# Layer 3's second product by Strassen's seven products, with the first product of the next group issued ahead of the last one of this group

## The chip, the cores and the metric

The kernel runs on one core of one Trainium2 chip. The metric is device time in microseconds (us), the median of several executions. The profiled execution of the kernel before has a span of 2726.4 us at a mean granted TensorE clock of 0.980.

Engines in the profile: PE is TensorE's matmuls, PEld its weight loads, DVE is VectorE, ACT is ScalarE, POOL is GpSimd, SP is SyncE; a "q" behind the name is that engine's instruction queue. L734 is line 734 of the kernel of that run.

## The reference

Four graph layers, each `x + layer(relu(layernorm(x)))`, on 128 graphs of 128 nodes and 256 features, in float32. Only the end of the fourth layer ("layer 3") changes:

```python
h = jax.nn.relu(_batchnorm(x @ W1.T + b1, g1, be1))   # x: 16384 rows; h: 16384 x 512
out = h @ W2.T + b2                                   # the "second product": 512 -> 256
out = _batchnorm(out, g2, be2)                        # statistics over all rows
```

Both batch normalizations need statistics over all rows, so the layer has three phases. The first product, which is merged into the main phase, writes its result `z` to HBM. The second product reads it back in 32 groups of 512 rows. The last phase (the "tail" below) normalizes, transposes, adds x and stores.

## The kernel before

The second product works on features by rows: a group `z` is 128 partitions x 4 feature blocks x 512 rows (1 MB). ScalarE applies the normalization and ReLU in place, TensorE does 2 x 4 matmuls of 512 columns, VectorE adds the bias and takes the statistics.

```python
EARLY = 6
x3p = pool("x3p", bufs=EARLY)              # x tiles for the tail, loaded ahead
zin = pool("zin", bufs=3)                  # three groups of z in SBUF
for n, g in enumerate(ORDER):
    z = ZT[g]
    for j in range(FC):                    # FC = 4
        nc.scalar.activation(z[j], z[j], AF.Relu, bias=sh1[:, j:j+1], scale=sc1[:, j:j+1])
    for i in range(DC):                    # DC = 2
        po = bank([P, T], f"po_{g}_{i}")   # T = 512 rows
        for j in range(FC):
            nc.tensor.matmul(po, bw2T[:, j, i*P:(i+1)*P], z[j], start=(j == 0), stop=(j == FC-1))
        nc.vector.tensor_scalar(O[g][:, i, :], po, b2_c[:, i:i+1], None, ALU.add)
        nc.vector.bn_stats(stats2[:, i, g, :], O[g][:, i, :])
    if n + 1 + AT_ONCE < NG: load_z(n + 1 + AT_ONCE)     # AT_ONCE = 3
    ...                                    # and sometimes one early x3 load
```

(Pool and slice notation shortened.) The weights `W2.T` are transposed in the preparation, parked in HBM as `BW2T`, and read back when the product starts.

## Time and profile before

| | before |
|---|---|
| time, median of 4 | 2728.28 us (2726.66 to 2731.1); 2727.35 of 3 when the prediction was made |
| first `h` of the kernel (end of the preparation) | 29.81 us |
| start of the second product on TensorE | 2424.80 us |
| second product, first to last matmul ("the block") | 221.95 us, 6.87 us a group |
| tail, from the block's end to the end | 79.65 us |

The last four rows cut the span into a start, a block and a tail, whose lengths add up to the span. The lines behind the table are in the prediction.

### The profile page before, as it was taken

Reading aid. Unit: us, or ns where it says so; the run is one execution under the profiler, and the core shown is the slowest. Engines: PE = TensorE matmul, PEld = TensorE weight load, DVE = VectorE, ACT = ScalarE, POOL = GpSimd, SP = SyncE. Lnnn points to the kernel's source line nnn. Section 1 sums busy time; section 2 is a strip of 40 time slices with the busy share of each in tenths; the row PEclk is TensorE's granted clock in tenths of the full one; section 3 lists DMA queues with packets and bytes.
Section 4 is the critical chain, followed back from the end, with each engine's and each line's share of the span. In section 5 each row is a group of like instructions: output and inputs, shape, how many; then the busy total and the mean of one; then the engine's idle time right before and its main releaser. Section 6 shows DMA issues by size and latency. Waiting matters only on the chain.

```text
span 2726.4 us, 38769 instructions
## 1 busy us (share of the span) xinstructions
PE 2611.4 (96%) x14703; PEld 2201.7 (81%) x14703; DVE 1806.0 (66%) x4528; ACT 1194.1 (44%) x2307; POOL 465.5 (17%) x484
## 2 busy tenths in 40 slices
PE   4899999999999999999999999999999999979994
PEld 2788888888888888888888888888888888954443
DVE  6666776676677766666777667677766665544445
ACT  2444444444444444444444444444444443334445
POOL 4111111111111111111111111111111111110001
PEclk6899999999999999999999999999999999989997
DMA  3000000000000000000000000000000000034449
GB/s 134 1 25 23 32 32 32 32 24 32 24 32 32 32 32 32 32 29 19 32 32 32 32 24 32 24 32 32 32 32 32 32 24 11 37 147 154 154 169 363
DMA packets 61756, 142.14 MB, mean 52 GB/s; under 512 B 4594, under 2 KB 39940, under 8 KB 57604
## 3 DMA queue, kind: packets, MB, share of 16 engines
q1 hardware_dynamic: 50224, 103.36, 10.7%
q0 software_dynamic: 9216, 33.56, 3.1%
q10 hardware_dynamic: 2132, 2.76, 0.3%
q8 instruction: 116, 1.90, 0.3%
q14 instruction: 68, 0.56, 0.1%
HBM read 73.08 MB, written 66.58 MB: 51 GB/s over the span
## 4 chain that ended last, share of the span: by engine, by line
PE 70%; DVE 20%; ACT 4%; POOL 3%; DMA 2%; issue 2%; ACTq 0%; DVEq 0%; POOLq 0%; SPq 0%
PE p_x L338 10%; PE po L714 8%; PE p_x L321 6%; PE p_z L338 4%; PE p_z L321 4%; PE pu_x L321 4%; PE pz_x L338 4%; DVE st L258 3%; DVE uT L280 3%; POOL rs L145 3%; PE pm L277 2%; PE p_y L338 2%; PE pg L277 2%; ACT h L267 2%; PE p_y L321 2%; PE ps L466 2%
## 5 line engine op out<-in xcount | busy, mean ns | idle before, releaser
L267 ACT ACTIVATE h<-x,sh,rs 128x256 f32<-128x256 f32 x512 | 265.9, 590 | 232.3 <-DVE sh L264 220.3
L145 POOL TENSOR_TENSOR rs<-rs,nhalf 128x4 f32<-128x4 f32 x128 | 135.1, 1056 | 1039.7 <-DVE rs L143 1039.7
L353 ACT COPY p_t<-p_x 128x512 f32<-128x512 f32 (+1 forms) x192 | 97.6, 508 | 343.1 <-PE p_x L338 340.9
L338 PE MATMUL p_x<-uT,w 128*128 128x256 f32 x1024 | 242.3, 379 | 0.0
L553 ACT ACTIVATE h2T<-h2T 128x512 f32<-128x512 f32 x192 | 119.9, 625 | 226.9 <-DVE h2T L552 226.9
L390 DVE SCALAR_TENSOR_TENSOR gs<-h,gw 128x256 f32<-128x256 f32 x384 | 203.8, 531 | 18.8 <-ACT h L267 6.8
L714 PE MATMUL po<-zi,bw2T 128*128 128x512 f32 x496 | 213.0, 592 | 0.0
L338 PEld LDWEIGHTS p_x<-uT,w 128*128 128x128 f32 x1024 | 189.7, 190 | 23.1
L258 DVE BATCH_NORM_STATS2 st<-x 128x6 f32<-128x256 f32 x512 | 191.0, 414 | 4.4 <-DMA x<-in_x_dram 2.2
L714 PEld LDWEIGHTS po<-zi,bw2T 128*128 128x128 f32 x496 | 94.2, 190 | 118.6 <-issue 108.1
L604 DVE TENSOR_TENSOR zo<-pz_z,pz_t 128x512 f32<-128x512 f32 x32 | 22.1, 691 | 185.6 <-PE pz_z L338 185.6
L707 ACT ACTIVATE zi<-zi,sh_bn,sc_bn 128x512 f32<-128x512 f32 x124 | 90.5, 802 | 116.7 <-DMA zi<-z 116.7
L718 DVE TENSOR_SCALAR o<-po,vecs 128x512 f32<-128x512 f32 x64 | 48.0, 750 | 128.7 <-PE po L714 128.7
L277 PEld LDWEIGHTS pmu<-a2T,u 128*128 128x128 f32 x1024 | 119.8, 192 | 15.0 <-PE pr L579 7.4
L338 PE MATMUL p_x<-uT,w_s 128*128 128x256 f32 x512 | 124.3, 385 | 6.1 <-DVE h2T L552 6.1
L321 PEld LDWEIGHTS p_x<-w,h2T 128*128 128x128 f32 x1024 | 124.3, 192 | 3.3
L338 PE MATMUL p_x<-us,w_s 128*128 128x256 f32 x512 | 126.0, 379 | 0.0
L321 PE MATMUL p_x<-w,h2T 128*128 128x128 f32 x1024 | 124.6, 275 | 0.0
L338 PE MATMUL p_y<-uT,w 128*128 128x256 f32 x512 | 121.1, 379 | 0.0
L338 PE MATMUL p_z<-us,w 128*128 128x256 f32 x512 | 121.0, 379 | 0.0
L338 PE MATMUL p_z<-us,w_s 128*128 128x256 f32 x512 | 121.0, 379 | 0.0
L277 PE MATMUL pmu<-a2T,u 128*128 128x128 f32 x1024 | 119.9, 275 | 0.0
(250 smaller groups left out, 5871.3 us busy)
## 6 DMA issues: line engine op xcount, KB each, us to landing
z<-zo SPq DMA_DIRECT2D x62, 512.0 KB, 2.6
zi<-z SPq DMA_DIRECT2D x31, 1024.0 KB, 4.8
x<-in_x_dram SPq DMA_DIRECT2D x32, 512.0 KB, 3.9
x<-x POOLq DMA_DIRECT2D x32, 512.0 KB, 3.0
x3i<-x POOLq DMA_DIRECT2D x32, 512.0 KB, 6.8
out_dram<-x3i SPq DMA_DIRECT2D x64, 256.0 KB, 6.6
w<-in_L_gnn_W_dram SPq DMA_DIRECT2D x1, 2048.0 KB, 11.1
bw<-in_L_gnn_W_dram ACTq DMA_DIRECT2D x2, 512.0 KB
```

The lines of the kernel that those rows point to most:

```text
L145: nc.gpsimd.tensor_tensor(dst, src, nhalf[:, : dst.shape[1]], ALU.pow)
L258: nc.vector.bn_stats(st[:, b, :], xt[:, b, :])
L267: nc.scalar.activation(h[:, b, :], xt[:, b, :], AF.Relu, bias=sh[:, b : b + 1], scale=rs[:, b : b + 1])
L277: nc.tensor.matmul(pm[:, b, :], src[:, b, c * P : (c + 1) * P], aT, start=True, stop=True)
L280: nc.vector.tensor_copy(dst[:, c, :], pm.rearrange("p b n -> p (b n)"))
L321: nc.tensor.matmul(pb[:, rr, :], a_r[r][:, c, rr * P : (rr + 1) * P], b_r[r][:, c, :wide], start=(first and rr == 0 and c == 0), stop=(c = ...
L338: nc.tensor.matmul(pb[:, jj, :], b_r[r][:, c, at : at + P], a_r[r][:, c, :], start=(first and jj == 0 and c == 0), stop=(c == nk - 1), ski ...
L353: nc.scalar.copy(t, pb)
L390: nc.vector.scalar_tensor_tensor(gs, h[:, b, :], 1.0, gw[:, i, :], ALU.mult, ALU.mult, accum_out=gl[:, b, i : i + 1],)
L553: nc.scalar.activation(dst, dst, AF.Relu)
L707: nc.scalar.activation(z[j], z[j], AF.Relu, bias=sh1[:, j : j + 1], scale=sc1[:, j : j + 1],)
L714: nc.tensor.matmul(po, bw2T[:, j, i * P : (i + 1) * P], z[j], start=(j == 0), stop=(j == FC - 1),)
```

## The change

Strassen's scheme in Winograd's form: A (the activations of one group) and B (the weights) are cut into 2 x 2 blocks, and seven products of half-sized blocks replace eight. Block sums of the weights are made once in the preparation (three extra blocks, `BW2S`, parked next to `BW2T`); block sums of the activations are made per group: S1 and S2 and the update of A12 on VectorE, the new A21 on GpSimd. The output needs sums of products too: four products are copied from PSUM by ScalarE, three added by VectorE. Of the four copies one is final and three are kept for a later sum: t1 behind product 0, t5 behind product 4, t2 behind product 5. The bias moves into the last normalization.

```diff
+    def second(g):
+        ...                                  # a11, a21, a12, a22: blocks of z; s1, s2: ex
+        a_r = a11, a12, a12, a22, s1, s2, a21
+        for j in range(FC):
+            nc.scalar.activation(z, z, AF.Relu, bias=..., scale=...)
+            yield
+        nc.vector.tensor_tensor(s1, a21, a22, ALU.add)
+        nc.gpsimd.tensor_tensor(a21, a11, a21, ALU.subtract)
+        nc.vector.tensor_tensor(s2, s1, a11, ALU.subtract)
+        yield
+        def product(r, pb, first):
+            for c in range(FC // 2):
+                nc.tensor.matmul(pb, BW2R[r][:, c, :], a_r[r][:, c, :], ...)
+            if r == 1:
+                nc.vector.tensor_tensor(a12, a12, s2, ALU.subtract)
+        ...                                  # put(): output copy or sum, statistics
+        yield from seven(product, put, [P, T // 2], f"po_{g}", zw)
     for n, g in enumerate(ORDER):
-        (ReLUs, 8 matmuls, bias, statistics: see above)
+        then = second(ORDER[n + 1]) if n + 1 < NG else iter(())
+        for _ in range(PREPARE):             # PREPARE = FC + 1
+            next(now)                        # a product of this group
+            next(then, None)                 # a ReLU, then the sums, of the next
+        next(then, None)                     # the next group's FIRST product
+        for _ in now: pass                   # this group's LAST product
+        now = then
```
```diff
-        nc.scalar.dma_start(BW2T, bw2t)
+        bw2s = prep.tile([P, 3, FC // 2, D // 2], FP, name="bw2s")
+        seven_of(bw2t, "bw2t", bw2s)         # four differences on GpSimd
+        nc.sync.dma_start(BW2T, bw2t)
+        nc.sync.dma_start(BW2S, bw2s)
...
-    EARLY = 6        (and 9 late x3 tiles)
+    EARLY, LATE = 4, 11
+    zw = pool("zw", bufs=2)                  # s1, s2 and the kept copies
```

`seven` runs the products in the order 0, 1, 4, 5, 2, 6, 3. Three PSUM banks serve them: x (0, then 5, 6 and 3 added on), y (1), z (4, then 2 added on). Product 2 reads the updated A12. And product 3 adds onto the bank that the output sum behind product 6 still reads; that is why the next group's product 0 is put between 6 and 3.

More of the change, by code (lines that the diff above doesn't have):

```diff
@@ L145, in inv_sqrt, with quarters, set_of, seven_of @@
         nc.gpsimd.tensor_tensor(dst, src, nhalf[:, : dst.shape[1]], ALU.pow)
+    def quarters(a):
+        k, t = a.shape[1] // 2, a.shape[2] // 2
+        return a[:, :k, :t], a[:, k:, :t], a[:, :k, t:], a[:, k:, t:]
+    def set_of(b, extra):
+        b11, b21, b12, b22 = quarters(b)
+        return b11, b21, b22, extra[:, 2], extra[:, 0], extra[:, 1], b12
+    def seven_of(b, name, extra=None):
+        b11, b21, b12, b22 = quarters(b)
+        if extra is None:
+            extra = weights.tile([P, 3, b.shape[1] // 2, b.shape[2] // 2], FP, name=f"{name}_s")
+        operands = set_of(b, extra)
+        t4n, t1, t2 = operands[3:6]
+        nc.gpsimd.tensor_tensor(t1, b12, b11, ALU.subtract)
+        nc.gpsimd.tensor_tensor(t2, b22, t1, ALU.subtract)
+        nc.gpsimd.tensor_tensor(t4n, b21, t2, ALU.subtract)
+        nc.gpsimd.tensor_tensor(b12, b22, b12, ALU.subtract)
+        return operands
     BW2T = scratch.tile([P, FC, D], FP, name="BW2T")
+    BW2S = scratch.tile([P, 3, FC // 2, D // 2], FP, name="BW2S")
     with tc.tile_pool(name="prep", bufs=1) as prep:
@@ L280, in mixed @@
             nc.vector.tensor_copy(dst[:, c, :], pm.rearrange("p b n -> p (b n)"))
-    def quarters(a):
-        k, t = a.shape[1] // 2, a.shape[2] // 2
-        return a[:, :k, :t], a[:, k:, :t], a[:, :k, t:], a[:, k:, t:]
-    def seven_of(b, name):
-        b11, b21, b12, b22 = quarters(b)
-        extra = weights.tile([P, 3, b.shape[1] // 2, b.shape[2] // 2], FP, name=f"{name}_s")
-        t1, t2, t4n = (extra[:, i] for i in range(3))
-        nc.gpsimd.tensor_tensor(t1, b12, b11, ALU.subtract)
-        nc.gpsimd.tensor_tensor(t2, b22, t1, ALU.subtract)
-        nc.gpsimd.tensor_tensor(t4n, b21, t2, ALU.subtract)
-        nc.gpsimd.tensor_tensor(b12, b22, b12, ALU.subtract)
-        return b11, b21, b22, t4n, t1, t2, b12
     def sums(engine, a, extra, s3=None):
@@ L344, in columns_by_half, with seven @@
         return product
-    def seven(product, put, shape, name):
+    def seven(product, put, shape, name, pool=None):
         def kept(pb, i):
-            t = w.tile(shape, FP, tag="kept", name=f"{name}_t{i}", bufs=6)
+            t = (pool or w).tile(shape, FP, tag="kept", name=f"{name}_t{i}", bufs=6)
             nc.scalar.copy(t, pb)
@@ L679 @@
     O = [keep.tile([P, DC, T], FP, name=f"o_{g}") for g in range(NG)]
-    EARLY = 6
+    EARLY, LATE = 4, 11
     x3p = ctx.enter_context(tc.tile_pool(name="x3p", bufs=EARLY, reuse_waits="tile"))
@@ L684 @@
     )
+    zw = zs.enter_context(tc.tile_pool(name="zw", bufs=2, side="right", reuse_waits="tile"))
     bw2T = keep.tile([P, FC, D], FP, name="bw2T")
     nc.scalar.dma_start(bw2T, BW2T)
+    bw2s = keep.tile([P, 3, FC // 2, D // 2], FP, name="bw2s_late")
+    nc.scalar.dma_start(bw2s, BW2S)
+    BW2R = set_of(bw2T, bw2s)
     ORDER = [LAST, *range(LAST)]
@@ L693, in load_z @@
         nc.sync.dma_start(z, Z[ORDER[n]])
-        ZT[ORDER[n]] = [z[:, j, :] for j in range(FC)]
+        ZT[ORDER[n]] = [z[:, :FC // 2, :], z[:, FC // 2 :, :]]
     def load_x3(g, pool, tag):
@@ L698, in load_x3, with put @@
         nc.gpsimd.dma_start(R[g], X3[g])
+    def second(g):
+        zl, zr = ZT[g]
+        ex = zw.tile([P, 2, FC // 2, T // 2], FP, tag="zs", name=f"zs_{g}")
+        a11, a21, a12, a22 = (z[:, :, i * T // 2 : (i + 1) * T // 2] for z in (zl, zr) for i in range(2))
+        s1, s2 = ex[:, 0], ex[:, 1]
+        a_r = a11, a12, a12, a22, s1, s2, a21
+        for j in range(FC):
+            z = ZT[g][j // 2][:, j % 2, :]
+            nc.scalar.activation(
+                z, z, AF.Relu, bias=sh1[:, j : j + 1], scale=sc1[:, j : j + 1],
+            )
+            yield
[5 more added lines that the diff above has]
+            for c in range(FC // 2):
+                nc.tensor.matmul(
+                    pb, BW2R[r][:, c, :], a_r[r][:, c, :],
+                    start=(first and c == 0), stop=(c == FC // 2 - 1), skip_group_check=True,
+                )
+            if r == 1:
+                nc.vector.tensor_tensor(a12, a12, s2, ALU.subtract)
+        done = []
+        def put(ij, pb, other):
+            i, j = ij
+            dst = O[g][:, j, i * T // 2 : (i + 1) * T // 2]
+            if other is None:
+                nc.scalar.copy(dst, pb)
+            else:
+                nc.vector.tensor_tensor(dst, pb, other, ALU.add)
+            done.append(j)
+            if done.count(j) == 2:
+                nc.vector.bn_stats(stats2[:, j, g, :], O[g][:, j, :])
+        yield from seven(product, put, [P, T // 2], f"po_{g}", zw)
     for n in range(1, 1 + AT_ONCE):
@@ L702 @@
     sc1, sh1 = bn_affine(stats1, FC, g1_c, be1_c, "bn1", b1_c)
-    ZT[LAST] = [z[:, jj, :] for z in ZT[LAST] for jj in range(2)]
+    PREPARE = FC + 1
+    now = second(LAST)
+    for _ in range(PREPARE + 1):
+        next(now)
     for n, g in enumerate(ORDER):
-        z = ZT[g]
-        for j in range(FC):
-            nc.scalar.activation(
-                z[j], z[j], AF.Relu,
-                bias=sh1[:, j : j + 1], scale=sc1[:, j : j + 1],
-            )
-        for i in range(DC):
-            po = bank([P, T], f"po_{g}_{i}")
-            for j in range(FC):
-                nc.tensor.matmul(
-                    po, bw2T[:, j, i * P : (i + 1) * P], z[j],
-                    start=(j == 0), stop=(j == FC - 1),
-                )
-            nc.vector.tensor_scalar(O[g][:, i, :], po, b2_c[:, i : i + 1], None, ALU.add)
-            nc.vector.bn_stats(stats2[:, i, g, :], O[g][:, i, :])
+        then = second(ORDER[n + 1]) if n + 1 < NG else iter(())
+        for _ in range(PREPARE):
+            next(now)
+            next(then, None)
+        next(then, None)
+        for _ in now:
+            pass
+        now = then
         if n + 1 + AT_ONCE < NG:
@@ L724 @@
     zs.close()
-    late = ctx.enter_context(tc.tile_pool(name="late", bufs=9, reuse_waits="tile"))
+    late = ctx.enter_context(tc.tile_pool(name="late", bufs=LATE, reuse_waits="tile"))
     def load_later(g):
-        load_x3(g, *((late, "x3l") if EARLY <= g < EARLY + 9 or g % 5 > 1 else (x3p, "x3")))
-    for g in range(EARLY, EARLY + 9):
+        load_x3(g, *((x3p, "x3") if g % (EARLY + LATE) < EARLY else (late, "x3l")))
+    for g in range(EARLY, EARLY + LATE):
         load_later(g)
-    sc2, sh2 = bn_affine(stats2, DC, g2_c, be2_c, "bn2")
+    sc2, sh2 = bn_affine(stats2, DC, g2_c, be2_c, "bn2", b2_c)
     for g in range(NG):
@@ L753 @@
             nc.sync.dma_start(out[at : at + 2].rearrange("b n d -> n b d"), x3[:, half, :])
-        if g + EARLY + 9 < NG:
-            load_later(g + EARLY + 9)
+        if g + EARLY + LATE < NG:
+            load_later(g + EARLY + LATE)
 _INS = [
```

## The prediction

> **What bounds the kernel now.** I read the page first (busy shares, the 40 slices, the chain of work that ended last), then the chain in order of time, the busy time of each engine by stretches, the groups of the lines concerned, and last the timeline of the three joints that the change touches: the preparation, the start of the second product, its end.
>
> From the page:
>
> ```profile
> PE 2611.4 (96%) x14703; PEld 2201.7 (81%) x14703; DVE 1806.0 (66%) x4528; ACT 1194.1 (44%) x2307; POOL 465.5 (17%) x484
> ...
> DMA  3000000000000000000000000000000000034449
> ```
>
> TensorE has work nearly everywhere, but the DMA row shows another regime in the last slices. The end of the chain in order of time separates the stages:
>
> ```profile
> 2416.91 1.80 DVE mv_bn L659 x2
> 2419.85 1.81 DVE mv_bn L659 x2
> 2424.80 221.95 PE po L714 x512
> 2650.93 15.69 ACT o L738 x23
> 2673.03 3.92 DMA x3i<-x
> ```
>
> So layer 3's second product is one unbroken TensorE block of 221.95 us, 8% of the span; behind it comes a tail of 76 us that ends in transfers. Everything ahead of 2416 us is the same code before and after, apart from the preparation. Busy time by stretches (columns PE, PEld, DVE, ACT, POOL, granted clock, DMA share, GB/s), one stretch inside the product and three of the tail:
>
> ```profile
> 2500.00:2550.00 50.00, 50.00 (x117) 22.04 (x116) 20.84 (x29) 21.76 (x30) 0.00 (x0) 1.00 0.41 147
> ...
> 2647.00:2654.00 7.00, 2.19 (x9) 1.74 (x10) 3.45 (x8) 3.07 (x5) 2.80 (x5) 0.76 0.78 270
> 2654.00:2664.00 10.00, 9.10 (x61) 7.94 (x60) 9.29 (x16) 10.00 (x15) 1.10 (x2) 0.83 0.90 297
> ...
> 2694.00:2704.00 10.00, 6.75 (x54) 6.19 (x52) 7.29 (x13) 2.19 (x4) 2.12 (x4) 0.95 1.06 404
> ```
>
> In the product TensorE is 100% busy at full clock, DVE and ACT 42 to 44%, POOL 0, DMA 41%: only TensorE binds. In the tail DMA binds: some 390 to 400 GB/s once saturated, but only 270 and 297 in its first 17 us. The groups of the product's line give the cost of one instruction:
>
> ```profile
> L714 PEld LDWEIGHTS po<-zi,bw2T x496: 190/190/190, 2433.3 to 2645.7; 128*128 128x128 f32 x166
> L714 PE MATMUL po<-zi,bw2T x496: 592/592/593, 2433.7 to 2646.1; 128*128 128x512 f32 x166
> ```
>
> (2646.1 - 2433.7)/495 = 0.429 us from one matmul to the next. A matmul of the code is two TensorE instructions (16 a group, 8 in the code), so a group takes 16 x 0.429 = 6.87 us.
>
> **What the Trainium skill says.** (1) "TensorE: Matmul & The Clock Gate", section "Back-to-back issue gap": the isolated warm gap grows with the moving columns, N/2.4 + 2.5 ns, 216 ns at 512. This trace has 429 ns at 512 columns of f32, twice that, so I take the proportionality and not the figure: eight 256-column f32 matmuls at 2227.91 us take 1.89 us, the last 0.379, hence (1.89 - 0.379)/7 = 0.216. Half the columns cost half. (2) The same page, "What's actually happening": after idle time the clock is halved for some 3.4 us. The trace agrees: after the 8 us gap ahead of the product the first weight loads are 0.86 us apart for 4.2 us. This loss stays. (3) "SBUF — State Buffer", "Who interferes with whom": a DVE instruction with two SBUF inputs and a GpSimd instruction that reads SBUF exclude each other, the later one waits. The trace agrees; beside POOL's sums at 2225.61 us the gate product takes 0.83 us in place of 0.42:
>
> ```profile
> 2225.45 0.41 DVE L390 SCALAR_TENSOR_TENSOR gs<-h,gw 128x256 f32<-128x256 f32 x1
> 2225.61 0.84 POOL L304 TENSOR_TENSOR gs<-gT 128x256 f32<-128x256 f32 x1 [5.61 <-DVE gT L280]
> ...
> 2226.77 0.82 DVE L390 SCALAR_TENSOR_TENSOR gs<-h,gw 128x256 f32<-128x256 f32 x1
> ```
>
> (4) "DMA: Bandwidth & Descriptors", "Where 436 GB/s comes from", puts HBM to SBUF at about 358 GB/s a core; the tail measures up to 404, so I use about 390.
>
> **The change part by part.**
>
> *TensorE, removed.* A group's 16 instructions of 512 columns become 7 products x 2 chunks x 2 passes = 28 of 256 columns: 28 x 0.2155 = 6.03 us against 6.87. If nothing else binds: 0.83 x 32 = 26.7 us. The weight load (0.190) still hides under the 0.216, as in the main phase.
>
> *ACT, added.* Four ReLUs (a run of four takes 2.92 us, 0.71 apart) plus four PSUM copies of 128x256 (0.35 each): about 4.2 us a group of 6.03.
>
> *DVE, replaced.* Gone: two bias additions of 0.75. New: three 128x512 sums (starts 0.60 apart) and three 128x256 sums from PSUM (0.42, or 0.35 apart); the two statistics (0.69) stay. About 4.1 us a group. No total binds; the order within a group does.
>
> *POOL, added.* One 128x512 difference a group, 1.27 us by its group in the main phase (L307).
>
> *The order.* Let product 6 of the last group end at 0; slots are 0.86 us: 0' to 0.86, 3 to 1.72, 1' to 2.58, 4' to 3.45, 5' to 4.31, 2' to 5.17, 6' to 6.03. On DVE: last output sum 0.09 to 0.50, statistics to about 1.1, s1' to 1.73 (in time for 4', which starts at 2.4), s2' to 2.33 (in time for 5'). POOL's difference needs s1' done, finds DVE in s2' (two SBUF inputs), and runs about 2.33 to 3.6. The update of a12', again two SBUF inputs, wants to start at 2.7 to 3.0 and is locked out until 3.6; it ends at 4.3. Product 2' should start near 4.15; it starts near 4.45. The loop from one product 6 to the next is then 4.45 + 0.17 (pipeline) + 2 x 0.86 = 6.35, not 6.03. The ACT order just passes: the copy t2' ends near 4.87, product 6' needs it near 4.9. I take **6.3 us a group**: (6.87 - 6.30) x 32 = **18.1 us saved**.
>
> *Transfers of z.* A buffer is now free when product 3 of its group ends, and its successor is read 6.03 + 0.4 = 6.4 us later. Before, the end of the group at about 2626.08 led to the ReLU at 2631.07: 5.0 us. There is slack of 1.4 us, so no charge.
>
> *Preparation.* The first h waits for a store of the preparation:
>
> ```profile
> 22.82 2.35 POOL L292 TENSOR_TENSOR w_s<-w 128x1024 f32<-128x1024 f32 x1
> ...
> 24.30 0.37 ACTq L237 DMA_DIRECT2D BW2T<-bw2t  x1
> ...
> 29.81 2.08 ACT L267 ACTIVATE h<-x,sh,rs 128x256 f32<-128x256 f32 x4 [12.04 <-DMA BW2T<-bw2t]
> ```
>
> Now four POOL sums of 128x256 (0.72 each here) go ahead of that store. POOL is busy until 25.17, so the trigger moves from 24.3 to about 25.2 + 2.9 = 28.1. The 5.4 us of landing before were queueing (DMA share 1.1 until 28 us, then 0.09); now two stores, 896 KB, go into an empty queue: 2 us of start and 0.9 MB at 370 GB/s, so about 32.4. The first h is 2.6 us later. TensorE binds from 60 us on, so this passes through: **+2.6 us**.
>
> *Joint at the end of the product.* The last product 3 has nothing between it and product 6: it waits for the sum that reads its bank, about 0.75. A copy of 0.37 takes the place of the 0.75 addition, -0.4; the bias in the last normalization adds two small DVE steps, 0.3. **+0.65 us**. At the start I charge nothing: in the half-clock stretch ACT keeps ahead.
>
> *Tail.* x3 loads before: 7 by 2426 us, 2 at 2633.5, 2 at 2640.4, 4 at 2647.3. After, the early pool has four buffers, not six, and by the sizes in the code the eleven late ones lie nearly all where z and its sums lie: about 1 goes 8 us ahead of the product's end, 2 go 2.6 us ahead, 8 at its end. That leaves some 4.75 loads, 2.5 MB, more for the tail. Unused bandwidth at the tail's start was (390 - 270) x 7 + (390 - 297) x 10 = 1.77 MB, which the eight waiting loads can fill. Net 0.7 MB or 1.9 us, and I allow 1 us for imperfect filling: **+3 us**.
>
> Sum: -18.1 + 2.6 + 0.65 + 3 = -11.9 us; 2727.35 - 11.9 = **2715.5 us**.
>
> **Rivals.** (a) *TensorE stays the only bound*: period 6.05, 26.2 us saved, and the rest as above: 2707. For it: the main phase runs such sevens with PE 99% busy. Against: there POOL and other streams have slack; here one stream is left. (b) *The DVE and POOL chain binds harder*: if POOL wins the lock first, s2' ends near 3.8, after product 5' wants it (3.28), and the wait repeats in every group: period 6.5 or more, 11.8 us saved or less: 2722. (c) *The gain is given back at the joints*: store, late x3 loads and tail at their worst, 5 + 6 us with 1.6 between: 2722 at period 6.3, near the time before if (b) holds too. (d) *Z transfers no longer land in time*, ACT stalls in order and the copies behind it: 0.5 us a group would cost 16 us. The 1.4 us of slack speaks against it.
>
> **Range and chances.** (a) with mild joints gives about 2705, (b) with bad joints 2724: that is the range. 2% is 54.5 us; even with all else free the gain is 26.7 us, and a loss of 54.5 would need a period above 8.2 us, more than any engine's total. So within 2% is nearly sure.
>
> **What would show it.** Right: the product's block near 202 us for 221.95, 896 matmuls about 0.216 apart with a pause of about 0.3 us a group ahead of product 2, waiting for a12 (DVE, then POOL); the first h near 32.4 us; x3 loads bunched at the product's end, DMA share 1 from there; the tail about 82 us against 79. Wrong: pauses ahead of product 5 or 6, ReLUs that wait for z, a block near 194 or above 210 us, an h that starts near 30, or a main phase of another length.

## The result and the profile after

The changed kernel takes **2716.15 us** (median of 4, 2715.21 to 2718.01) against 2728.28 us (median of 4). The ratio is 0.9955, 95% interval 0.9938 to 0.9973, well inside 2%.

The cut into stages, with the prediction's terms beside it:

| stage | before | after | change | predicted |
|---|---|---|---|---|
| start to first matmul of the block | 2424.80 | 2429.71 | +4.9 | +2.6 |
| block | 221.95 | 204.78 | -17.2 | -18.1 + 0.75 = -17.35 |
| tail | 79.65 | 79.9 | +0.3 | +3 - 0.1 = +2.9 |
| span of the profiled run | 2726.4 | 2714.4 | -12.0 | -11.9 |

(The joint's 0.65 of the prediction is split here: 0.75 lies before the last matmul, -0.4 and +0.3 behind it.) The sum is right to 0.1 us. The block is right to 0.2 us by the terms of the sum; the block "near 202 us" that the prediction names as its sign does not follow from them (221.95 - 17.35 = 204.6) and was 2.8 us short. The outer terms are each off by 2.3 to 2.6 us, in opposite directions. Start and tail are read from one trace each, and they scatter: over the ten runs with these x3 tiles, the changed kernel among them, the tail is 79.1 to 82.0 us, mean 80.4.

**The product.** The groups of the product's line in the changed kernel give the price of an instruction and what TensorE waited for (us, times):

```profile
L734 PE MATMUL po_x<-zi,bw2T x248: 379/379/379, 2437.2 to 2632.5; 128*128 128x256 f32 x124
...
  ACT zo L723: 16.6, 3
  ACT po_t L363: 13.1, 34
```

The view counts matmuls and weight loads apart, so one pause can stand in it twice. The 16.6 us in three waits belong to the first group. What is new is 13.1 us of waiting for ScalarE's copies out of PSUM (`po_t`), 10.5 of weight loads in 23 waits and 2.6 of matmuls in 11. The chain of waits in order of time (start, length, what) over one turn of two groups shows where the copies get late:

```profile
2522.09 4.81 DMA zi<-z
...
2527.00 0.17 ACT zi L723
...
2527.72 0.34 ACT po_t L363
...
2528.69 0.36 ACT o L747
...
2529.08 0.03 DVE stats L752
...
2529.69 0.69 DVE zi L739
2530.37 0.35 ACT po_t L363
...
2530.77 1.13 PE po_z L734 x4
2531.90 2.60 PE po_x L734 x12
...
2534.63 4.80 DMA zi<-z
```

The chain runs from one load of z to the next and repeats after 2534.63 - 2522.09 = 12.54 us, which is two groups of 6.27 us (mean from the fifth group to the 28th: 6.30). The load lands at 2526.90, the first ReLU (L723) of that buffer runs, then the copy t1 (L363) and the output copy (L747). From there two paths of the same length lead on: two more ReLUs and t5 on ScalarE, and statistics (L752) and the update of A12 (L739) on VectorE. The profile goes by the second, but t5 also starts directly behind the ReLUs, 0.705 us after the last one began, in nearly every group. In the groups that pause, product 2 (`po_z<-zi`) starts 0.05 us behind t5 and 0.41 us behind the update: t5 is the last, and the update is late for the same cause. At the end of product 3 the buffer is free and the next load goes out. In the source the first ReLU stands behind t1 and behind the output copy; the compile-time scheduler put it ahead of t1. ScalarE waited 53.5 us in 26 waits for `zi<-z`, each time holding the copies behind it. "ReLUs that wait for z" was one of the prediction's own signs of being wrong.

**The preparation.** The timeline around the first `h`:

```profile
29.60 0.72 POOL L163 TENSOR_TENSOR bw2s<-bw2t 128x256 f32<-128x256 f32 x1
30.28 2.34 POOL L165 TENSOR_TENSOR w_s<-w,w_s 128x1024 f32<-128x1024 f32 x1
...
33.95 0.72 POOL L165 TENSOR_TENSOR bw2s<-bw2t,bw2s 128x256 f32<-128x256 f32 x1
...
34.70 0.34 SPq L263 DMA_DIRECT2D BW2S<-bw2s  x1
...
38.26 2.07 ACT L293 ACTIVATE h<-x,sh,rs 128x256 f32<-128x256 f32 x4 [19.26 <-DMA BW2S<-bw2s]
```

The first `h` is 38.26 - 29.81 = 8.45 us later (predicted 2.6). The four small sums of `bw2s` were not put ahead of GpSimd's large ones but between them and behind them, so the store's trigger stands at 34.70 us, not at 28.1. Only 4.9 of the 8.45 us reach the product. Most of the rest is seen in the timelines: before, the first gate product on VectorE took 2.58 us and the next seven 0.75 to 1.36 us each beside GpSimd's sums, up to 41 us; after, the first took 3.00 us, and from 41.9 us on they take 0.42, since GpSimd is done by then. The twelfth starts at 44.19 us before and 48.37 after, only 4.2 us later.

**The tail.** Busy time by stretches (us, then PE, PEld, DVE, ACT, POOL busy, granted clock, DMA share, GB/s), the end of the product and the 7 us behind it, first of the kernel before, then of the changed one:

```profile
2639.00:2646.70 7.70, 7.70 (x19) 3.07 (x17) 3.91 (x5) 0.00 (x0) 1.05 (x2) 1.00 0.35 136
2646.70:2653.70 7.00, 1.92 (x9) 1.50 (x9) 3.38 (x8) 2.77 (x4) 2.80 (x5) 0.78 0.74 254
```
```profile
2627.00:2634.50 7.50, 6.97 (x32) 5.46 (x30) 4.55 (x9) 1.49 (x4) 3.32 (x7) 1.00 0.80 289
2634.50:2641.50 7.00, 1.34 (x5) 0.94 (x6) 3.08 (x10) 2.60 (x5) 3.34 (x6) 0.82 1.01 387
```

Six x3 loads went out together at 2627.14, right behind GpSimd's last difference, 7.3 us before the product's end. So the transfers ran at 289 GB/s where before, in the last 7.7 us of the product, they ran at 136, and at 387 in the next 7 us where before they ran at 254 (270 in the stretch of the prediction, which begins 0.3 us later). I take it that the bandwidth that lay idle paid for the two x3 tiles fewer at hand; no run tests this alone.

### The profile page after: what moved, and what is told of

Its sections match the earlier page's. It is cut to its first block, busy times and chain, and to the rows that moved or that the text cites. A ratio compares the mean times of both kernels' runs of the same rounds, so it can differ in the third digit from the quotient of the medians.

```text
span 2714.4 us, 40129 instructions
## 1 busy us (share of the span) xinstructions
PE 2591.6 (95%) x15087; PEld 2270.4 (84%) x15087; DVE 1853.5 (68%) x4659; ACT 1231.4 (45%) x2435; POOL 518.6 (19%) x520
## 4 chain that ended last, share of the span: by engine, by line
PE 67%; DVE 20%; ACT 5%; POOL 3%; DMA 3%; issue 2%; ACTq 0%; DVEq 0%; SPq 0%
PE p_x L348 10%; PE p_x L331 6%; PE p_z L348 4%; PE p_z L331 4%; PE pu_x L331 4%; PE pz_x L348 4%; DVE st L284 3%; PE po_x L734 3%; DVE uT L306 3%; POOL rs L145 3%; PE pm L303 2%; PE p_y L348 2%; PE pg L303 2%; ACT h L293 2%; PE p_y L331 2%; PE ps L476 2%
## 5 line engine op out<-in xcount | busy, mean ns | idle before, releaser
L363 ACT COPY p_t<-p_x 128x512 f32<-128x512 f32 (+1 forms) x192 | 97.5, 508 | 343.4 <-PE p_x L348 341.2
L723 ACT ACTIVATE zi<-zi,sh_bn,sc_bn 128x512 f32<-128x512 f32 x124 | 97.4, 812 | 57.9 <-DMA zi<-z 53.5
L593 POOL DMA_DIRECT2D x<-x x32 | 19.8, 620 | 521.7 <-DVE x L590 521.7
L529 ACT ACTIVATE u<-u 128x512 f32<-128x512 f32 x96 | 60.5, 630 | 119.0 <-DVE u L528 119.0
L348 PEld LDWEIGHTS p_x<-uT,w_s 128*128 128x128 f32 x512 | 94.6, 190 | 23.4 <-DVE h2T L562 11.7
```

Source lines behind the costliest of these rows:

```text
L348: nc.tensor.matmul(pb[:, jj, :], b_r[r][:, c, at : at + P], a_r[r][:, c, :], start=(first and jj == 0 and c == 0), stop=(c == nk - 1), ski ...
L363: nc.scalar.copy(t, pb)
L723: nc.scalar.activation(z, z, AF.Relu, bias=sh1[:, j : j + 1], scale=sc1[:, j : j + 1],)
```

## The experiments

The theory after the result, called C: the period in the changed kernel is set by the loop of the z load, not by the shared port of VectorE and GpSimd as predicted. Theory L: the predicted lock. Theory P: the order of GpSimd's sums delays `h`. "Block" is measured in each run's trace as above; the other times are medians. The kernel before ran on the same chip and took 2728.1 to 2729.5 us.

**1. prep_on_vector** moves the four small sums to VectorE.

```diff
-        nc.gpsimd.tensor_tensor(t1, b12, b11, ALU.subtract)     # and three more
+        engine.tensor_tensor(t1, b12, b11, ALU.subtract)        # engine=nc.vector for bw2t
```

> The changed kernel, but the four sums that prepare the second product's weights run on VectorE, not GpSimd. In the changed kernel they stand among the sums of W2 in GpSimd's queue, the store behind them is issued at 34.0 us and the first h starts at 38.26 us, against 24.3 and 29.81 before; yet the main phase starts only 5.0 us later. Theory P (GpSimd's queue holds the store): the sums take four times 0.42 us right behind the last copy, the store goes near 24.5 us, the first h starts at 30 to 31.5 us, everything from 60 us on is 4 to 5 us earlier, near 2711.5 us in all; the product's block stays at 204.8 us. Rival (the size of the store, 896 KB for 512, holds h): h stays above 35 us and the time falls by less than 1.5 us.

Measured: 2713.51 us (2711.31 to 2715.57), ratio 0.9942 (0.9927 to 0.9957). The block stays at 204.86 us and starts 3.3 us earlier than in the changed kernel, at 2426.45. `h` starts at 33.75, still behind the store of BW2S: on VectorE the sums took 0.83 to 2.56 us each in place of 0.72, locked beside GpSimd's large ones. P is right in kind. How much is to be read with care, since the block's start moves with any new order: in the ten runs with the sums on GpSimd, the changed kernel among them, it lies between 2427.7 and 2431.1, mean 2429.2, and in the three with the sums on VectorE between 2425.7 and 2426.7, mean 2426.3. The order cost 2.9 us by these means. The expected 4 to 5 were too many; the sums on VectorE, 0.83 to 2.56 us where 0.42 were expected, are part of that.

**2. z_four_buffers and z_three_early_two.** Four buffers for z, paid for with two early x3 tiles; the second run is the control, with the same x3 tiles and three buffers.

```diff
-    EARLY, LATE = 4, 11          # both runs
+    EARLY, LATE = 2, 13
-    zin bufs=3;  AT_ONCE = 3     # z_four_buffers only
+    zin bufs=4;  AT_ONCE = 4
```

> The changed kernel with four buffers for z in place of three; the early x3 pool gives up the room (2 early and 13 late in place of 4 and 11). Theory Z: the product's groups take 6.28 us because ScalarE, which works in order, stands at a ReLU whose z has not landed, so that the copy of the fifth term behind it comes late and product 2 waits for it. With a fourth buffer z is issued one group sooner: the weight loads' wait for that copy (13.1 us in sum) falls below 3 us and the block from the first product to the last falls from 204.8 to 197 or 198 us. Theory L, that of the prediction (GpSimd's difference locks VectorE out of the update of a12): the block stays within 1 us of 204.8. The tail is read against the run with three buffers and the same x3 pools.

> The changed kernel with 2 early and 13 late x3 buffers in place of 4 and 11, z with three buffers as before: the control for the run with four z buffers, and a test of the tail's price. The block stays at 204.8 us. If a load that is no longer issued early costs its bytes at the saturated rate, the tail grows by 2 x 0.524 MB / 0.39 MB per us = 2.7 us, from 79.9 to 82.6; if the late loads start early enough to fill the transfer engines, it stays within 1 us.

Measured: 2719.46 us (ratio 0.9964, 0.9949 to 0.9979) with four, 2717.16 us (0.9957, 0.9941 to 0.9974) with three. Blocks: 204.62 and 204.99 us. **The fourth buffer gained nothing**, against my expectation, and ScalarE still waited 53.4 us for the loads. The compiled order shows why: with one more buffer free, the scheduler moved each group's ReLUs one more group ahead, so that the first ReLU for a buffer stood again just where its load lands, in front of the copies. The control's tail is 81.85 us against 79.9, one trace each. The three runs with two early x3 tiles have tails of 81.9 to 83.8 us, mean 83.1, the ten with four 79.1 to 82.0, mean 80.4, so two early tiles are worth some 2 to 3 us of tail; the control's time, 2717.16 us, does not show it beyond the noise.

**3. t5_on_vector** takes the copy that product 2 waits for away from ScalarE.

```diff
-            nc.scalar.copy(t, pb)
+            if i == 5 and pool is not None:
+                nc.vector.tensor_copy(t, pb)
+            else:
+                nc.scalar.copy(t, pb)
```

> The changed kernel, but the copy of the fifth term of the second product is made by VectorE (0.42 us a group there), so that it no longer stands behind a ReLU in ScalarE's queue. Theory Z: product 2 no longer waits for that copy, the block falls from 204.8 to 197 to 199 us although ScalarE still waits for z. Rival R: z itself cannot come faster than one group in 6.3 us (buffer free, issue, landing), and then another product takes over the wait and the block stays above 203 us. Theory L (VectorE and GpSimd are the bound): the block grows, since VectorE gets 0.42 us more a group.

Measured: 2716.46 us, ratio 0.9954 (0.9939 to 0.9969), block 204.78 us. TensorE now waits 14.0 us in 35 waits for the same copy on VectorE, where it stands behind the update of A12, the statistics and an output sum: product 4 ended at 2522.18 in one group, the copy began at 2522.96. In this run the scheduler left the ReLUs where the source has them, so no ReLU waits for a load any more, and the update of A12 takes 0.69 us, free of the lock. So neither C nor L holds the period, which is 6.27 us all the same: the wait moved to VectorE's queue, a third limit at the same height. The number is the one that rival R gave, but not for R's reason.

**4. act_source_order** keeps ReLUs and copies on ScalarE in source order; nothing else changes.

```diff
-            nc.scalar.copy(t, pb)
+            copy = nc.scalar.copy(t, pb)
+            if pool is not None:
+                tc.keep_in_program_order(copy)
...             # the same around the ReLU and the output copy
```

> The changed kernel with three z buffers, but ScalarE's instructions of the second product are kept in the order of the source: the first ReLU of the group after next stands behind the copy to O, and the copies t5 and t2 stand ahead of the second and third ReLU. In the changed kernel the scheduler moved the first ReLU ahead of the copy t1, so that ScalarE waits there for z, and the chain of waits shows a loop over two groups of 12.55 us: product 3 ends, z is loaded (4.8 us), ReLU, t1, ReLU, copy to O, two ReLUs, t5, product 2, product 3. The run with four buffers did not test this, since the scheduler moved the ReLUs one group further ahead and the same wait came back. Theory C (that loop sets 6.28 us a group): with the ReLU later by about 1.4 us z has landed, product 2 no longer waits, the block falls from 204.8 to 196 to 198.5 us, the time by 6 to 8 us. Theory L (the prediction: GpSimd's difference locks VectorE out of the update of a12): this is the very order that the prediction worked with, the group takes 6.3 us or more and the block stays at 203 to 207 us.

Measured: 2718.49 us, ratio 0.9962 (0.9947 to 0.9977), block 207.3 us, period 6.42. ScalarE no longer waits for a load in this stage at all, and TensorE's waits for copies fall from 13.1 to 1.1 us. So the load loop is gone, and the time is no better: theory L appears. In the timeline:

```profile
2521.02 1.28 POOL L730 TENSOR_TENSOR zi<-zi 128x512 f32<-128x512 f32 x1 [5.14 <-DVE zs L729]
...
2521.31 1.53 DVE L731 TENSOR_TENSOR zs<-zs,zi 128x512 f32<-128x512 f32 x1
...
2523.37 0.67 DVE L741 TENSOR_TENSOR zi<-zi,zs 128x512 f32<-128x512 f32 x1
...
2524.15 0.73 PEld L736 LDWEIGHTS po_z<-zi,bw2T 128*128 128x128 f32 x4 [0.46 <-issue]
```

Here the statistics stand between S1 and S2 on VectorE. GpSimd's difference starts in that gap, and S2 (L731) takes 1.53 us; it took 0.69 in the changed kernel. The update of A12 (L741) then ends at 2524.04, and product 2's first weight load starts 0.11 us later, TensorE having stood for 0.46 us. The profile calls that wait "issue"; the timeline names it.

**5. not_ahead** issues the next group's product 0 behind this group's product 3.

```diff
-        next(then, None)
         for _ in now:
             pass
+        with tc.issue_after(ENDS[g].ins):    # ENDS[g]: the group's last matmul
+            next(then, None)
```

> The changed kernel, but TensorE's first product of the next group is held behind the last product of this one (order alone, no wait on data). Undoes one half of the change. Product 3 then stands right behind product 6 and waits for the sum that reads product 6's bank: in the last group, where nothing stands between, TensorE waits 0.52 us and the weight loads 0.92. If that wait comes in every group and nothing else takes it up: 32 times 0.5 to 0.75, the block grows from 204.8 by 16 to 24 us, and the change as a whole gains nothing. Rival: the loop over z and ScalarE has that much slack already spent in waits ahead of product 2, so the new wait only takes the place of that one and the block grows by 8 to 14 us.

Measured: 2732.13 us, ratio 1.0013 (0.9996 to 1.003), block 220.96 us, period 6.83. For the output sums TensorE's matmuls wait 16.6 us and its weight loads 29.4, both once a group. The block grew by 16.2 us, the low end of what was expected. Without the "ahead" in its title the change is worth nothing: in this order of the banks seven products run hardly faster than the plain eight's 6.87 us a group.

**6. a21_on_vector** (one look, one run, state unknown) moves GpSimd's difference to VectorE, so that nothing can be locked, and leaves the load loop.

```diff
-        nc.gpsimd.tensor_tensor(a21, a11, a21, ALU.subtract)
+        nc.vector.tensor_tensor(a21, a11, a21, ALU.subtract)
```

> The changed kernel, but the difference of a21 runs on VectorE in place of GpSimd. Theory L: no GpSimd instruction is left to lock VectorE out, VectorE takes 0.6 us more a group, the block falls below 203 us. Theory C: GpSimd is not on the loop, and VectorE has slack: the block stays within 1 us of 204.8.

Measured: 2715.77 us, once; block 203.1 us, with 8.6 us of waits for copies and 7.1 for output sums. Taking the lock away alone gains 1.7 us of block, in one trace: less than theory L asked for to the letter (below 203) and more than theory C allowed (within 1 us of 204.8).

**7. z4_pinned, z_halves, halves_prep.** Two more attempts on the load loop, and the second with the preparation of run 1. z4_pinned is z_four_buffers with each ReLU held behind t1 of the group before; z_halves loads z as two tiles of 512 KB.

```diff
+            with tc.issue_after(T1[f"po_{ORDER[before]}"]):   # z4_pinned
                 nc.scalar.activation(z, z, AF.Relu, ...)
```
```diff
-        z = zin.tile([P, FC, T], FP, tag="zi", ...)             # z_halves
-        nc.sync.dma_start(z, Z[ORDER[n]])
+        for h in range(2):
+            z = zin.tile([P, FC // 2, T], FP, tag=f"zi{h}", ...)
+            nc.sync.dma_start(z, Z[ORDER[n]][:, 2 * h : 2 * h + 2, :])
```

> Four buffers for h1, as in z_four_buffers, but the ReLUs of a group may not be issued before the first copy of the group before it, so that the compile-time order cannot spend the fourth buffer on more lead again. Theory C (in the changed kernel the period is set by the loop load of h1, first ReLU, two copies queued behind it, second product, release of the buffer): the load now has a whole group of slack, the wait of the products for the copies on ScalarE (13.1 us in the changed kernel) falls under 4 us, the period from 6.28 to 6.03 to 6.10 us and the block from 204.8 to 197 to 200 us; with two x3 tiles fewer loaded early the tail is longer by about 2 us (the control z_three_early_two showed 1.95), so the time is about 3 to 5 us under z_three_early_two, 2712 to 2714 us. Rival L (once the load is out of the way the shared port of VectorE and GpSimd sets the period, as it did with ScalarE in source order): the block is 206 to 208 us, products wait for VectorE's update of the block A12, and the time is 2719 to 2721 us.

> The load of h1 cut in two halves with their own tiles, three of each, same memory in all: the half with the blocks A11 and A21 is free as soon as the product that reads A21 last is through, and the first ReLU waits for 512 KB in place of 1 MB. Theory C: the loop over two groups (12.55 us) loses the landing time of half a transfer and more, 2 to 3 us, so 1 to 1.5 us per group, more than the 0.25 us by which the period exceeds the products' own time; the period becomes 6.03 to 6.10 us, the block 197 to 200 us, the waits of products for copies on ScalarE fall from 13.1 to under 4 us, and the time falls by 5 to 8 us against the changed kernel, to 2708 to 2711 us. Rival L: the wait passes to VectorE's update or its statistics, the block stays at 203 to 208 us and the time within 3 us of 2716.

> z_halves and prep_on_vector together, the candidate for beating both kernels. Theory C with theory P (the order of the four small sums on GpSimd behind the large ones delays h): the gains add, the main phase starts 2.5 to 3.5 us earlier than in the changed kernel and the block is that of z_halves; 2705 to 2708 us. If L holds for z_halves, only the 3 us of the preparation remain: 2712 to 2715 us.

Measured: 2744.64 us (ratio 1.0061, 1.0046 to 1.0076), 2740.95 us (1.0046, 1.0031 to 1.0061) and 2736.54 us (1.003, 1.0013 to 1.0047). Both expectations fell, and not by a little: the blocks are 229.8, 226.5 and 227.4 us, longer than the kernel before's 221.95. In z4_pinned ScalarE waits for no load in this stage, and yet a group takes 7.14 us. Its chain of waits:

```profile
2510.07 1.15 PE po_x L739 x4
...
2513.24 0.82 ACT zi L728
...
2515.19 1.63 DVE zs L734
2516.82 0.35 DVE o L754
...
2517.21 1.15 PE po_x L739 x4
```

Product 3 waits for an output sum (L754), which stands on VectorE behind S2 (L734, 1.63 us under the lock), which waits for the last ReLUs, which stand on ScalarE behind an output copy, which waits for product 3 of the group before. Pinning one pair moved the ReLUs late enough to close this longer ring. In z_halves two pieces alternate, about 7.1 us a group in the mean: one through VectorE (output sum, then the ReLU released, S1, statistics, S2 at 1.44 us, statistics, update of A12, product 2), and one that still passes a load of z (3.72 us), a ReLU and t5. ScalarE still waits 39.0 us for loads. Neither is a fair test of C, since each also gave the other engines a new order. What they show is how much that order is worth: z4_pinned's block is 25 us longer than that of z_four_buffers, which differs in order alone, and that is more than the change itself brings.

**8. both_orders** is act_source_order with one pair exchanged per group: the statistics now stand ahead of S1, so S2 follows S1 directly.

```diff
-        nc.vector.tensor_tensor(s1, a21, a22, ALU.add)
+        tc.keep_in_program_order(nc.vector.tensor_tensor(s1, a21, a22, ALU.add))
...             # the same around S2 and bn_stats
```

> act_source_order with one pair of VectorE's instructions in each group exchanged and nothing else: the second sum s2 now stands right behind the first one s1, with the statistics before both, in place of between them. Three buffers, 4 and 11 x3 tiles as in the changed kernel. Theory: two loops bound the period, the load loop of h1 (broken by ScalarE in source order) and the lock loop (GpSimd takes the shared port in the gap between s1 and s2, s2 takes 1.53 us, the update of A12 ends 0.46 us after TensorE could go on). With the pair together s2 should take 0.69 us, GpSimd's difference 1.6 us, and the update of A12 end 0.2 to 0.6 us earlier against TensorE; the period goes from 6.42 to 6.05 to 6.20 us, the block from 207.3 to 196 to 201 us, the time from 2718.5 to 2707 to 2712 us. Rival: as in z4_pinned and z_halves, whatever is moved on these in-order engines only opens another loop; then s2 is short but the update of A12 is locked out by GpSimd in its turn, the period stays at 6.35 to 6.5 us and the time at 2716 to 2720 us.

Measured: 2717.32 us (ratio 0.9958, 0.9941 to 0.9974), block 204.42 us, period 6.30. The load loop is gone (no ReLU waits for a load) and S2 is short, but the update pays, as the rival had it:

```profile
2520.24 0.69 DVE L731 TENSOR_TENSOR zs<-zs,zi 128x512 f32<-128x512 f32 x1
...
2520.43 1.63 POOL L730 TENSOR_TENSOR zi<-zi 128x512 f32<-128x512 f32 x1 [4.67 <-DVE zs L729]
...
2521.45 1.16 DVE L741 TENSOR_TENSOR zi<-zi,zs 128x512 f32<-128x512 f32 x1
...
2521.91 0.37 ACT L363 COPY po_t<-po_z 128x256 f32<-128x256 f32 x1 [0.64 <-PE po_z L736]
...
2522.73 0.73 PEld L736 LDWEIGHTS po_z<-zi,bw2T 128*128 128x128 f32 x4 [0.39 <-ACT po_t L363]
```

GpSimd waits for S2 and takes the port right behind it, so the update of A12 (L741) takes 1.16 us and ends at 2522.61. The weight load of product 2 follows 0.12 us later. (The profile puts the wait down to the copy t5, which was done at 2522.28; it is not the later of the two.) This is the prediction's own chain, to the instruction, at the 6.3 us that it took.

**9. no_lock_prep** is both_orders with GpSimd's difference on VectorE directly behind the update, so that GpSimd does no arithmetic in the product, plus prep_on_vector.

```diff
-        nc.gpsimd.tensor_tensor(a21, a11, a21, ALU.subtract)
...
-                nc.vector.tensor_tensor(a12, a12, s2, ALU.subtract)
+                tc.keep_in_program_order(nc.vector.tensor_tensor(a12, a12, s2, ALU.subtract))
+                tc.keep_in_program_order(nc.vector.tensor_tensor(a21, a11, a21, ALU.subtract))
```

> both_orders, with GpSimd's difference for A21 moved to VectorE right behind the update of A12, so that GpSimd does no arithmetic in this stage and nothing can lose the shared port; and, in the preparation, the four small sums on VectorE as in prep_on_vector, whose effect lies before the block and is read apart. In both_orders the load loop and the long s2 are gone, and what is left is the update of A12 at 1.16 us against 0.67 us alone, after which the second product's weights can only be loaded in the open (its four matmuls take 1.10 in place of 0.86 us). Theory (two loops, no third): the update takes 0.67 us and ends at least 0.4 us earlier against TensorE, the first load of h1 in front of ScalarE keeps over 1 us of slack, no product waits more than 3 us in all for ScalarE's copies outside the first groups, the period goes from 6.30 to TensorE's own 6.03 to 6.08 us, the block from about 205 to 196 to 199 us, and with 3 us from the preparation the time from 2717 to 2705 to 2709 us. Rival (another loop opens, now VectorE's own queue with one more instruction): the period stays at 6.2 to 6.4 us, the block at 202 to 206 us and the time at 2712 to 2716 us, all that is gained being the preparation.

Measured: **2704.78 us** (median of 5, 2702.66 to 2705.51), ratio to the kernel before 0.9913 (0.9899 to 0.9926). All that TensorE waits for in the whole product:

```profile
  ACT zo L725: 16.6, 3
  DVE o L751: 1.4, 2
```

and the chain of waits is TensorE alone, with a period of 2509.97 - 2503.92 = 6.05 us:

```profile
2503.92 0.86 PE po_z L735 x4
2504.79 2.59 PE po_x L735 x12
...
2509.97 0.86 PE po_z L735 x4
```

The update takes 0.67 us. The block is 196.38 us, 8.0 less than in both_orders; it starts at 2425.74, 3.3 earlier; the tail is 80.8 us against 81.2. This beats both kernels: 12.5 us under both_orders by the medians, about 11 under the changed kernel (each against its own rounds of the kernel before).

Blocks of the runs side by side:

| run | load loop | lock | period us | block us | time us |
|---|---|---|---|---|---|
| changed kernel | yes | off the path | 6.27 (mean 6.30) | 204.78 | 2716.15 |
| t5_on_vector | no | off the path; t5 late in VectorE's queue | 6.27 | 204.78 | 2716.46 |
| act_source_order | no | S2 long | 6.42 | 207.3 | 2718.49 |
| both_orders | no | update long | 6.30 | 204.42 | 2717.32 |
| a21_on_vector (one run) | yes | no | mixed, mean 6.28 | 203.1 | 2715.77 |
| no_lock_prep | no | no | 6.05 | 196.38 | 2704.78 |

**What follows.** Two limits lay one behind the other at nearly the same period, 6.27 and 6.30 to 6.42 us, both only just above TensorE's own 6.03. Removing one uncovers the other, so each alone moves the time by 2.4 us or less, in either direction; removing both shortens the block by 8 us at once. So C and L are both real, and each bounds the kernel where the other is gone; for C without L there is only the single look at a21_on_vector. They are not the only limits at this height: in t5_on_vector neither holds, and VectorE's queue gives 6.27 us. The update of A12 also became pinned in order in the last run, and the difference moved behind it, so the run doesn't separate "no GpSimd" from "a21 later"; both take the lock away.

## Why the prediction was right, and where it was right by luck

**TensorE's own time** was right: 28 instructions at 0.2155 us were to make 6.03 us, and no_lock_prep shows 6.04 to 6.05 when nothing else binds. Rival (a)'s period was 6.05.

**The order** (the period of 6.3) was right in size and wrong in mechanism. The shipped kernel does pause ahead of product 2, as predicted, but for the copy t5; A12 was complete 0.36 us earlier: its scheduler placed S1, S2 and GpSimd's difference so early in the period that the update was not locked. The predicted chain is real; it came out in both_orders, at 6.30 us. Rival (b), in which GpSimd gets the port first, came out in act_source_order, at 6.42 us (I had said 6.5 or more).

**Transfers of z** is the step that failed in the product: "There is slack of 1.4 us, so no charge", and rival (d) dismissed on the same ground. The slack was worked out for ReLUs in source order. The compile-time scheduler moved the first ReLU ahead of t1, to where the load just lands, and used the slack up. Rival (d)'s mechanism is the one that ran, at 0.24 to 0.27 us a group in place of 0.5. The copies can't go around the waiting ReLU: the Trainium skill, "TensorE: Matmul & The Clock Gate", section "Step-by-step: what each phase is for", says that PE is the only engine that reorders. The trace agrees for ScalarE: the copy t1 of 0.34 us starts at 2527.72, behind a ReLU that stood waiting for a load until 2527.00.

**The preparation** failed in one step: "POOL is busy until 25.17, so the trigger moves from 24.3 to about 25.2 + 2.9 = 28.1". The small sums were interleaved with 2.34 us ones, and the trigger came at 34.70. `h` was 8.45 us late, of which 4.9 reached the product (4.4 by the mean of the ten starts). So "this passes through" was wrong as well, as a rule of one to one: some 4 us were won back ahead of 60 us, where the gate products no longer met GpSimd's sums. The landing was right: `h` came 4.25 us behind the first of the two stores' triggers (34.01), where 4.3 were allowed. (The "2 us of start" in it is an estimate without its source; the 1 MB loads of z, 4.8 us each, give about 2.0 at 370 GB/s.)

**The tail** was mis-sized by the step "by the sizes in the code the eleven late ones lie nearly all where z and its sums lie", which let eight loads go at the product's end. Six went 7.3 us before it. The mechanism named there, unused bandwidth at the tail's start, was right and larger than allowed for: 289 and 387 GB/s where 136 and 254 had flowed. The term measured +0.3, not +2.9; by the mean tail of the ten runs it is +0.8.

**The joint**: product 3 of the last group waits 0.52 us for the sum that reads its bank (predicted 0.75).

So the total of -11.9 against a measured -12.0 is partly luck: +2.3 in the preparation and -2.6 in the tail cancelled, and the period was right because two rings have nearly the same length, of which the prediction had only the one that did not run.

## What to carry to other kernels

When work for three engines is woven into one stream, compute the length of every ring that returns to the same buffer or bank (load, ReLU, copy, product; sum, lock, update, product), and not the busy time per engine alone: the longest ring is the period, and removing one shows only the step down to the next. A compile-time scheduler can spend spare buffers on moving work earlier, as z_four_buffers shows, so slack that is read from source order need not be there, and more buffers may gain nothing: check the compiled order of the in-order engines before counting on it. If a wait merely changes its name after a fix, look for the second ring and take both away in one run. And when a fix moves an instruction to another engine, check in its trace what the scheduler moved along with it: t5_on_vector changed one copy, and the order on ScalarE changed too.

## What the Trainium skill lacked or had wrong

- "SBUF — State Buffer", "Who interferes with whom", says that issue order decides who blocks, and the runs confirm it, but it has no price for float32 sums under the lock. Here a 128x512 VectorE sum takes 0.69 us free and 1.53 us behind GpSimd's 1.28 us difference; with VectorE first, GpSimd takes 1.63 and VectorE's next sum of two SBUF inputs 1.16 in place of 0.67. The lock can pass to the instruction after next.
- "TensorE: Matmul & The Clock Gate", "Step-by-step: what each phase is for", has weight loads pulled ahead of running matmuls. It lacks a warning that the compiled program can forgo this: product 2's weights don't depend on A12, yet in both_orders their load began only when the update had ended (2522.73 behind 2522.61), and its four matmuls took 1.10 us in place of 0.86. The trace lists semaphore waits in the weight loads' own queue for this line (`PEldq EVENT_SEMAPHORE`, 104 of them), so I take it that the program put the wait there; it does not show that the hardware could not have loaded earlier.
- "DMA: Bandwidth & Descriptors", "Where 436 GB/s comes from", lets about 358 GB/s bind between HBM and SBUF. The tail of the kernel before ran at 404 GB/s over 10 us, that of the changed one at 387 over 7 us. The page's figure is half of what two cores share; the program here runs on one core, so it may hold when both are busy, which no run tests.
- I found no page on what a compile-time order does to buffer depth: a fourth z buffer left the block at 204.62 us (204.99 with three), and other orders of nearly the same instructions (in the shortest, one moved to VectorE) made it 196.38 to 229.8.
